# Selective scan's step: other places for products, sums, du and the pieces beside

## The chip, the cores and the metric

The kernel runs on one core of a Trainium2 chip. The core has five engines that work side by side, each through its own queue in order: TensorE (PE, matmuls), VectorE (DVE), ScalarE (ACT), GpSimd (POOL) and SyncE (SP, which only issues DMAs here). The metric is the time of one execution on the device, in microseconds (us). A profile of one execution lists the instructions of every engine with start, duration and the event that ended the idle time before each.

## The reference, cut to what matters

Eight images of 64 x 64 x 96 pass four layers. Layers 0 and 2 are selective scans (the subject here), layer 1 is a scan in chunks, layer 3 a resampling with a small network ("slow layer" in the kernel). The core of layers 0 and 2, for four directions (k) over the L = 4096 points, 192 channels (d) and 16 states (n):

```python
delta = softplus(dts + dt_projs_bias)
def step(h, inp):
    ut, dt, bt, ct = inp
    dA = jnp.exp(dt[..., None] * A4)
    dBu = (dt * ut)[..., None] * bt[:, :, None, :]
    h = h * dA + dBu
    y = jnp.einsum('bkdn,bkn->bkd', h, ct)
    return (h, y)
```

Directions 1 and 3 read the image transposed, directions 2 and 3 backwards; the four y are added.

## The kernel before

`selective_scan` cuts a direction into 8 chunks of 512 points, so a layer has 32 steps (direction, chunk). A step has six units (n = 0 to 5) of 32 channels. In a unit's tiles the 128 partitions are 32 channels x 4 states, and four groups of 512 points (the other states) lie behind each other: 2048 elements per partition. Units 0 to 2 hold channels 0 to 95 (half 0), units 3 to 5 the others. There are 8 images x 2 layers x 32 steps = 512 steps.

What a unit needs, by function:

- `spread` (L821): PE copies one unit's 32 rows of du = delta * u onto the 128 partitions, into the PSUM tile pu (one buffer, tag "misc").
- `with_b` (L828): db = pu * B. Units 0, 1, 3, 4 on DVE from pu; units 2 and 5 on POOL from du2, a copy of du that comes by DMA.
- `decays` (L840): ACT makes exp(delta * A) for two groups into PSUM tile da0 or da1 (p = 0, 1).
- `scan` (L854): DVE's scan over two groups, from da and db to h. It frees da for the next unit's decays.
- `leave` (L871): ACT saves the last column as state, POOL multiplies h by C in place. `enter` (L811): ACT puts the earlier state into db.
- `total_y` (L885): PE adds, for the three units of a half, over the partitions: first the earlier y (or the skip term, L890), then 12 products with `red` (L900), each to 32 of 96 columns by q. ACT copies the result to y (L1001 or L1011).

`prepare` (L720) makes the tiles of a step ahead, as a generator that `prepare_part` moves on by one part: pv on PE (L733); ACT's copy to raw (L738); pv on PE (L743); copy (L747), DMA bcd, and the four DMAs that make b; softplus on ACT and two DMAs dd; four DMAs dx of half 0 and four of c; du on POOL (L785 transposed, L791 else), DMA dud and four DMAs du2; dx of half 1. `Beside` (L619) runs the slow layer of the image before as pieces: `begin` issues a piece's matmuls into a PSUM tile, `end` has ACT take it away. There are 119 pieces in layer 0 and 116 in layer 2, so 3 or 4 per step (`quota`), from the second image on. The first image has none. Both pv, the sums and most pieces share one PSUM tile, tag "py".

The order is written out by hand in the loop over t from L971: what stands there is the order in each engine's queue. Before, DVE's order over a step was (S for a scan, B for a product): unit 0 S S B, units 1 and 2 S S, S S B, unit 3 S S B, unit 4 S S, unit 5 S S B. `with_b` for units 2 and 5, on POOL, follows the first scan two units earlier. Each sum of y was issued whole (at n = 0 for units 3 to 5 of the step before, at n = 3 for units 0 to 2), in this order:

```python
for g in range(NSG):
    for q in range(3):
        nc.tensor.matmul(
            turn_back(py[32 * q : 32 * q + 32, :], wh, LC), red, cut(hs[q][:, g, :], wh),
            start=False, stop=(g == NSG - 1))
```

## Time and profile before

| | |
|---|---|
| median of 3 runs | 26653.47 us (26631.27 to 26673.9) |
| the profiled execution | 26693.06 us, its span 26691.2 us |
| mean granted TensorE clock | 0.794 |
| instructions | 282273 |
| ACT, L847 (decays), 12288 | 8478.8 us busy, 690 ns each |
| DVE, L832 (with_b), 2048 | 4643.3 us busy, 2267 ns each |
| POOL, L785 and L791 (du), 256 each | 2885 and 2381 ns each |
| PE, L826 (spread), 4096 records | 2940.8 us busy, 805 ns each |
| DMA | 2836.59 MB, mean 106 GB/s |

A group's line in the profile names line, engine, operation, output and inputs with their shapes and the number of instructions; behind the bar stand the busy time of the group, the mean duration of one in ns, and the idle time of the engine before them with what ended it. In PE's groups 128*32 means active rows * columns. PEclk is the share of the full TensorE clock that was granted. In a timeline each row is start, duration, engine, line, operation and tiles; SPq rows are issues of DMAs.

### The profile page before, as it was taken

Reading aid. Unit: us, or ns where it says so; the run is one execution under the profiler, and the core shown is the slowest. Engines: PE = TensorE matmul, PEld = TensorE weight load, DVE = VectorE, ACT = ScalarE, POOL = GpSimd, SP = SyncE. Lnnn points to the kernel's source line nnn. Section 1 sums busy time; section 2 is a strip of 40 time slices with the busy share of each in tenths; the row PEclk is TensorE's granted clock in tenths of the full one; section 3 lists DMA queues with packets and bytes.
Section 4 is the critical chain, followed back from the end, with each engine's and each line's share of the span. In section 5 each row is a group of like instructions: output and inputs, shape, how many; then the busy total and the mean of one; then the engine's idle time right before and its main releaser. Section 6 shows DMA issues by size and latency. Waiting matters only on the chain. (4 is left out here: it accounts for less than half of the span.)

```text
span 26691.2 us, 282273 instructions
## 1 busy us (share of the span) xinstructions
PE 21984.9 (82%) x90981; PEld 8484.0 (32%) x90981; DVE 23982.3 (90%) x16689; ACT 16407.9 (61%) x29921; POOL 21235.6 (80%) x7928
## 2 busy tenths in 40 slices
PE   6796788888888878888888887888888888788888
PEld 2151222422224222242223422234222342223424
DVE  9989999898998989889898898988989889898896
ACT  5656566565665656556565565655656556565564
POOL 8949898497975979759797697976979769796694
PEclk7787777877778777787778877788777887778878
DMA  5515454154541545425453254532545325453352
GB/s 125 122 35 129 120 129 109 41 132 123 131 107 47 131 123 132 102 50 133 123 132 97 58 132 123 133 90 62 132 123 132 85 68 133 123 133 78 75 132 68
DMA packets 1678115, 2836.59 MB, mean 106 GB/s; under 512 B 434473, under 2 KB 477769, under 8 KB 1672033
## 3 DMA queue, kind: packets, MB, share of 16 engines
q1 hardware_dynamic: 1660000, 2812.23, 43.3%
q8 instruction: 731, 11.98, 0.2%
q10 hardware_dynamic: 16640, 6.29, 0.1%
q14 instruction: 744, 6.09, 0.1%
HBM read 2390.02 MB, written 427.49 MB: 106 GB/s over the span
## 5 line engine op out<-in xcount | busy, mean ns | idle before, releaser
L862 DVE TENSOR_TENSOR_SCAN h<-da,db 128x1026 f32<-128x1026 f32 x6144 | 13745.7, 2281 | 744.8 <-ACT da L847 378.5
L883 POOL TENSOR_TENSOR h<-h,c 128x2048 f32<-128x2048 f32 x3072 | 12743.1, 4172 | 968.2 <-ACT state L878 528.3
L900 PE MATMUL py<-h,cst 128*32 128x512 f32 x24576 | 5344.6, 749 | 473.0 <-POOL h L883 472.6
L847 ACT ACTIVATE da<-dx,a0s 128x512 f32<-128x512 f32 x6144 | 4239.6, 690 | 1548.8 <-DVE h L862 1373.0
L847 ACT ACTIVATE da<-dx,a2s 128x512 f32<-128x512 f32 x6144 | 4239.2, 690 | 1546.5 <-DVE h L862 1375.0
L832 POOL TENSOR_TENSOR db<-du,b 128x2048 f32<-128x2048 f32 x1024 | 4661.3, 4552 | 306.7 <-DMA du<-dud 226.5
L832 DVE TENSOR_TENSOR db<-pu,b 128x2048 f32<-128x2048 f32 x2048 | 4643.3, 2267 | 141.6 <-PE pu L826 138.2
L826 PE MATMUL pu<-du,cst 32*128 32x512 f32 x4096 | 2940.8, 805 | 1455.7 <-DVE db L832 927.4
L900 PEld LDWEIGHTS py<-h,cst 128*32 128x32 f32 x24576 | 1217.5, 133 | 4997.2 <-issue 3829.7
L826 PEld LDWEIGHTS pu<-du,cst 32*128 32x128 f32 x4096 | 735.2, 223 | 3145.9 <-DVE db L832 1580.8
L743 PE MATMUL pv<-u,wk 96*128 96x512 f32 x2048 | 1290.5, 762 | 388.1 <-ACT raw L738 388.1
L506 PE MATMUL ps<-s,w3as 96*128 96x512 f32 x1344 | 1069.4, 888 | 641.7 <-ACT sf L513 258.9
L1349 ACT ACTIVATE sg<-sg 128x768 f32<-128x768 f32 x1024 | 819.6, 800 | 862.2 <-PE sg L1333 862.2
L890 PE MATMUL py<-y,cst 96*96 96x512 f32 x1536 | 1306.1, 946 | 9.0 <-ACT y L1011 5.7
L733 PE MATMUL pv<-u,wk 96*96 96x512 f32 x2048 | 1200.9, 716 | 59.6 <-DVE u L281 27.4
L1303 POOL TENSOR_TENSOR ce<-ec,cr 112x512 f32<-112x512 f32 x256 | 521.5, 2037 | 754.9 <-ACT ec L1301 736.6
L1381 DVE TENSOR_TENSOR wt<-wt,cbm 128x768 f32<-128x768 f32 x1024 | 990.6, 1001 | 128.9 <-ACT wt L1350 128.1
L878 ACT COPY state<-h 128x4 f32<-128x4 f32 x3072 | 588.6, 192 | 796.5 <-DVE h L862 788.2
L526 PE MATMUL ps<-w3bs,sf 128*128 128x96 f32 x5376 | 1071.5, 356 | 0.0
L314 POOL TENSOR_SCALAR xn<-xs,sb 96x512 f32<-96x512 f32 x192 | 204.8, 1069 | 997.9 <-PE pz L319 440.8
L526 PEld LDWEIGHTS ps<-w3bs,sf 128*128 128x128 f32 x5376 | 992.9, 270 | 0.0
L738 ACT COPY raw<-pv 96x512 f32<-96x512 f32 x512 | 297.6, 581 | 970.1 <-PE pv L733 943.5
(238 smaller groups left out, 29900.9 us busy)
## 6 DMA issues: line engine op xcount, KB each, us to landing
dx<-dd SPq DMA_DIRECT2D x4096, 192.0 KB
b<-bcd SPq DMA_DIRECT2D x2048, 256.0 KB
c<-bcd SPq DMA_DIRECT2D x2048, 256.0 KB
du<-dud SPq DMA_DIRECT2D x2048, 128.0 KB
dd<-raw SPq DMA_DIRECT2D x1024, 192.0 KB
dud<-du SPq DMA_DIRECT2D x512, 128.0 KB
xd<-xs SPq DMA_DIRECT2D x256, 192.0 KB
cr<-bcd SPq DMA_DIRECT2D x1536, 32.0 KB
```

The source lines that it names most:

```text
L506: nc.tensor.matmul(ps, w3as[:, m * 128 : (m + 1) * 128], live["x2"], start=True, stop=True)
L526: nc.tensor.matmul(po, live["f"][m][:, at : at + 128], w2q[:, m, :], start=False, stop=(m == 2),)
L733: nc.tensor.matmul(pv[:DM], weights[k][:, hi, 128:], uv[hi], start=(hi == 0), stop=(hi == 1))
L743: nc.tensor.matmul(pv, weights[k][:, hi, :128], uv[hi], start=(hi == 0), stop=(hi == 1))
L826: nc.tensor.matmul(pu, sel[rows, :], m["du"][rows, n // 3, :], start=True, stop=True)
L832: (nc.gpsimd if pool else nc.vector).tensor_mul(groups(m["db", n]), (m["du2"][:, n // 3, :] if pool else m["pu"]) .unsqueeze(1) .to_broadc ...
L847: nc.scalar.activation(dst[:, g, :LC], made[i]["dx"][n // 3][:, n % 3, :], AF.Exp, scale=av4[:, k, n, gs : gs + 1],)
L862: nc.vector.tensor_tensor_scan(made[i]["h", n][:, at][:, way], das[p][:, rev : 2 * SEG + rev][:, way], made[i]["db", n][:, at][:, way], 0. ...
L883: nc.gpsimd.tensor_mul(h, h, made[i]["c"])
L890: nc.tensor.matmul(py, skip[:, hf, :] if k == 0 else ident[:DM, :DM], near((u if k == 0 else y)[:, hf, :], wh, c * LC, LC), start=True, st ...
L900: nc.tensor.matmul(turn_back(py[32 * q : 32 * q + 32, :], wh, LC), red, cut(hs[q][:, g, :], wh), start=False, stop=(g == NSG - 1),)
L1381: nc.vector.tensor_mul(it["wt"], it["wt"], m["cbm"][:, j : j + 1, :].to_broadcast([128, RK, Q]),)
```

## The change

`prepare` gets one more `yield`, between du and its DMAs (dud, du2), and so has nine parts. du is computed in unit 2 (`leave(t, n == 2)`), its DMAs are issued at the end of unit 5. `with_b` can do half of the groups. The loop is written anew: in every unit a product, or half of one, stands between the two scans (unit 0: B of unit 1; units 1 and 2: the halves for unit 3; unit 3: B of unit 4; units 4 and 5: the halves for the next unit 0). POOL's products for units 2 and 5 come first in units 0 and 3. `total_y` becomes a generator with the loops over q and g changed about: q = 0 and 1 are issued first, at the start of units 0 and 3, q = 2 after a `spread` later in the same unit. The sum's copy stands before `decays` in units 1 and 4. The pieces beside are begun and ended elsewhere, now all in the "py" tile; softplus stands in the middle of unit 0, the first pv at the end of unit 4 with its copy.

```diff
@@ -790,6 +790,7 @@
                 else:
                     nc.gpsimd.tensor_mul(du, raw[:DM], u[:, :, at : at + LC])
                 m["du"] = du
+                yield
                 dud = dp.tile([32, 2, LC], F32, name="dud")
                 nc.sync.dma_start(dud, du[64:96])
                 m["du2"] = du2 = tp.tile([128, 2, LC], F32, name="du2")
@@ -825,16 +826,17 @@
                 m["pu"] = pu = pmp.tile([128, LC], F32, name="pu", tag="misc")
                 nc.tensor.matmul(pu, sel[rows, :], m["du"][rows, n // 3, :], start=True, stop=True)
 
-            def with_b(t):
+            def with_b(t, part=slice(None)):
 
                 m, n = made[t // units], t % units
                 pool = n % 3 == 2
+                out, b = groups(m["db", n])[:, part], m["b"][:, part]
                 (nc.gpsimd if pool else nc.vector).tensor_mul(
-                    groups(m["db", n]),
+                    out,
                     (m["du2"][:, n // 3, :] if pool else m["pu"])
                     .unsqueeze(1)
-                    .to_broadcast([128, NSG, LC]),
-                    m["b"],
+                    .to_broadcast([128, out.shape[1], LC]),
+                    b,
                 )
 
             def decays(t, p):
@@ -894,18 +896,20 @@
                     start=True,
                     stop=False,
                 )
-                hs = [groups(made[i].pop(("h", 3 * hf + q))) for q in range(3)]
-                for g in range(NSG):
-                    for q in range(3):
+                for q in range(3):
+                    h = groups(made[i].pop(("h", 3 * hf + q)))
+                    for g in range(NSG):
                         nc.tensor.matmul(
                             turn_back(py[32 * q : 32 * q + 32, :], wh, LC),
                             red,
-                            cut(hs[q][:, g, :], wh),
+                            cut(h[:, g, :], wh),
                             start=False,
                             stop=(g == NSG - 1),
                         )
+                    if q == 1:
+                        yield
                 py = py.rearrange("p (h w) -> p h w", h=64) if wh else py
-                return near(y[:, hf, :], wh, c * LC, LC), py
+                yield near(y[:, hf, :], wh, c * LC, LC), py
 
             going = {}
 
@@ -943,7 +947,7 @@
                 prepare_part(0)
             conv_half(5, 1, pmp, "misc")
             conv(w, y, u, (8, 24), 0)
-            for _ in range(2):
+            for _ in range(3):
                 prepare_part(0)
             conv_half(6, 0, pyp, "py")
             for t in range(3):
@@ -967,65 +971,91 @@
                 prepare_part(1)
             conv(w, y, u, (40, 48), 0)
             with_b(0)
+            spread(1)
             other = Beside(ops)
+            low, high = slice(0, 2), slice(2, 4)
             for t in range(total + 2):
                 n, i = t % units, t // units
-                ahead = t + 1 < total
+                live, ahead = t < total, t + 1 < total
+                if t >= total:
+                    if n == 0:
+                        adding = total_y(i - 1, 1)
+                        next(adding)
+                        sums = next(adding)
+                    else:
+                        nc.scalar.copy(*sums)
+                    continue
                 quota = (i + 1) * len(ops) // len(steps) - i * len(ops) // len(steps)
-                if n == 2 and quota > 1:
+                assert quota <= 4
+
+                if n == 0:
+                    with_b(t + 2)
+                    if i > 0:
+                        adding = total_y(i - 1, 1)
+                        next(adding)
+                elif n == 3:
+                    adding = total_y(i, 0)
+                    next(adding)
+                elif n == 5:
+                    prepare_part(i + 2)
+                scan(t, 0)
+                if n == 1 and t > 1:
+                    nc.scalar.copy(*sums)
+                elif n == 4:
+                    nc.scalar.copy(*sums)
+                if ahead:
+                    decays(t + 1, 0)
+                if n == 0:
+                    with_b(t + 1)
+                    prepare_part(i + 1)
+                elif n == 1:
                     other.begin(pyp, "py")
-                if n in (0, 3) and ahead:
-                    spread(t + 1)
-                elif n == 1 and t + 2 < total:
+                    with_b(t + 2, low)
+                elif n == 2:
+                    other.end()
+                    with_b(t + 1, high)
                     spread(t + 2)
-                if n == 0 and i > 0:
-                    sums = total_y(i - 1, 1)
+                    if quota > 3:
+                        other.begin(pyp, "py")
                 elif n == 3:
-                    sums = total_y(i, 0)
+                    with_b(t + 2)
+                    with_b(t + 1)
+                    if t + 3 < total:
+                        spread(t + 3)
+                    sums = next(adding)
                 elif n == 4:
-                    if quota > 3:
-                        other.begin(pmp, "misc")
+                    if quota > 2:
+                        other.begin(pyp, "py")
                     if t + 2 < total:
+                        with_b(t + 2, low)
+                elif n == 5:
+                    prepare_part(i + 2)
+                    if ahead:
+                        with_b(t + 1, high)
                         spread(t + 2)
+                scan(t, 1)
+                if n == 0:
+                    spread(t + 3)
+                    if i > 0:
+                        sums = next(adding)
+                elif n in (1, 4):
+                    other.end()
+                leave(t, n == 2)
+                if ahead:
+                    decays(t + 1, 1)
+                if n == 2:
+                    other.end()
+                if t + 3 < total:
+                    enter(t + 3)
+                if n == 1:
+                    if quota > 1:
+                        other.begin(pyp, "py")
+                    prepare_part(i + 1)
+                elif n == 4:
+                    prepare_part(i + 2)
                     prepare_part(i + 2)
                 elif n == 5:
-                    prepare_part(i + 2)
-                if t < total:
-                    scan(t, 0)
-                    if n % 3 == 0 and t + 2 < total:
-                        with_b(t + 2)
-                if ahead:
-                    decays(t + 1, 0)
-                if n == 1:
-                    if t > 1:
-                        nc.scalar.copy(*sums)
-                    if t < total:
-                        other.begin(pyp, "py")
-                elif n == 2:
-                    other.end()
-                    if quota > 2:
-                        other.begin(pyp, "py")
-                elif n == 3:
-                    other.end()
-                elif n == 4:
-                    nc.scalar.copy(*sums)
-                    other.end()
-                if t < total:
-                    scan(t, 1)
-                    leave(t, n == 3)
-                if t + 3 < total:
-                    enter(t + 3)
-                if ahead:
-                    decays(t + 1, 1)
-                    if (n + 1) % 3 != 2:
-                        with_b(t + 1)
-                if n in (1, 2):
-                    other.end()
-                    if n == 2 and quota > 4:
-                        other.begin(pyp, "py")
-                if n in (4, 5):
-                    prepare_part(i + 2)
-                if n in (0, 1, 5):
+                    prepare_part(i + 1)
                     prepare_part(i + 1)
             other.flush()
             assert other.at == len(ops)
```

## The prediction

> **What bounds the kernel now.** I read the page's busy line and its groups first.
>
> ```profile
> PE 21984.9 (82%) x90981; PEld 8484.0 (32%) x90981; DVE 23982.3 (90%) x16689; ACT 16407.9 (61%) x29921; POOL 21235.6 (80%) x7928
> ...
> L862 DVE TENSOR_TENSOR_SCAN h<-da,db 128x1026 f32<-128x1026 f32 x6144 | 13745.7, 2281 | 744.8 <-ACT da L847 378.5
> L883 POOL TENSOR_TENSOR h<-h,c 128x2048 f32<-128x2048 f32 x3072 | 12743.1, 4172 | 968.2 <-ACT state L878 528.3
> L900 PE MATMUL py<-h,cst 128*32 128x512 f32 x24576 | 5344.6, 749 | 473.0 <-POOL h L883 472.6
> ...
> L832 POOL TENSOR_TENSOR db<-du,b 128x2048 f32<-128x2048 f32 x1024 | 4661.3, 4552 | 306.7 <-DMA du<-dud 226.5
> ```
>
> There are 512 steps of six units. From first scan to first scan of the next step they are 36.25 us apart in the first image's two scan layers (64 steps, no pieces beside) and 37.4 in the other fourteen (448 steps). DVE works 12 scans at a pitch of 2.24 and 4 products at 2.25 = 35.9 us per step. POOL works 6 x 4.13 + 2 x 4.5 + 2.85 (L785) or 2.33 (L791) = 36.6 or 36.1, mean 36.35. DVE's idle time before L862 and L832 is 744.8 + 141.6 = 886 us in all. So the best that any reordering can do is POOL's mean: 448 x (37.4 - 36.35) = 470 us. PE is not the bound, but its price is what the change alters, so I read two more views. The timeline of PE's weight loads and matmuls over one sum of y:
>
> ```profile
> 1028.84 3.62 PE L900 MATMUL py<-h,cst 128*32 128x512 f32 x20 [2.37 <-POOL h L883]
> ...
> 1030.16 0.12 PEld L900 LDWEIGHTS py<-h,cst 128*32 128x32 f32 x3 [0.31 <-issue]
> 1030.59 0.12 PEld L900 LDWEIGHTS py<-h,cst 128*32 128x32 f32 x3 [0.31 <-issue]
> 1031.02 0.11 PEld L900 LDWEIGHTS py<-h,cst 128*32 128x32 f32 x1 [0.31 <-issue]
> 1031.45 0.11 PEld L900 LDWEIGHTS py<-h,cst 128*32 128x32 f32 x1 [0.32 <-issue]
> ```
>
> Each product has two records (24576 over 512 x 24). Three records, one for each q and its 32 columns, start together every 0.43 us. Two of the q had run ahead here while the third waited for h, and so the last loads come singly: still 0.43 us apart. Three side by side cost what one alone costs. The second view is windows of 3.41 us, the grid on which the trace's clock changes:
>
> ```profile
> core 0: us, PE busy (x) PEld busy (x) DVE busy (x) ACT busy (x) POOL busy (x), PEclk, DMA share, GB/s
> 1006.46:1009.87 3.41, 3.41 (x7) 0.59 (x8) 3.41 (x2) 1.38 (x2) 3.41 (x2) 0.50 1.01 220
> 1009.87:1013.28 3.41, 3.41 (x15) 0.77 (x12) 3.31 (x3) 1.58 (x4) 3.41 (x1) 0.50 0.03 5
> 1013.28:1016.70 3.42, 1.91 (x13) 0.49 (x8) 3.42 (x3) 1.90 (x3) 3.42 (x3) 1.00 0.00 0
> ...
> 1061.07:1064.48 3.41, 3.41 (x5) 0.88 (x4) 3.37 (x3) 2.26 (x7) 3.41 (x2) 0.50 0.08 19
> 1064.48:1067.90 3.42, 3.42 (x11) 0.54 (x13) 3.32 (x2) 3.36 (x6) 3.42 (x2) 0.50 0.59 172
> 1067.90:1071.31 3.41, 3.41 (x23) 0.81 (x17) 3.22 (x3) 3.35 (x5) 3.41 (x2) 1.00 0.82 189
> ```
>
> PE is busy throughout the first two and the fourth and fifth. Only the second and fifth, where three L900 ran at a time, are followed by full clock; the first and fourth held mainly L826 (32 rows) and L890. I counted all 7812 such windows, weighting each matmul by active rows x columns over 128 x 128. At half clock, none of 125 windows that one stream filled, but with under 45% of the array, was followed by full clock; 46% of those at 54 to 62% were, and 99% above 74%. At full clock, 71% of the 38 filled by one stream of about a quarter of the array kept it. At half clock everything doubles: such loads are then 0.85 us apart.
>
> **The change, part by part.**
>
> *Products.* Two of four DVE products per step become halves. A half costs between 1.13 (half of L832's 2.27) and 1.21 us (L333, 1024 elements from PSUM); I take 1.18, nearest to L333. Two splits add 0.2 us, so DVE has 36.1, hidden under POOL's 36.35. Uncovered: 100 us over 512 steps. Evenly spread products give ACT at least 3.4 us between the scans that it serves instead of 2.24; this is what could win the 470 us.
>
> *du and its DMAs.* du moves on POOL from before unit 3's product to before unit 2's, so that db of unit 5 comes one du (2.85) later. Its DMAs do not follow: dud and du2 (5 issues) move from unit 3 to the end of unit 5, on SP behind bcd and b of the step after. The SP timeline:
>
> ```profile
> 1016.42 0.31 SPq L794 DMA_DIRECT2D dud<-du  x1
> 1018.38 1.71 SPq L797 DMA_DIRECT2D du<-dud  x4
> 1023.50 0.30 SPq L749 DMA_DIRECT2D bcd<-raw  x1
> 1025.14 1.74 SPq L756 DMA_DIRECT2D b<-bcd  x4
> 1026.93 1.84 SPq L774 DMA_DIRECT2D dx<-dd  x4
> ```
>
> From the copy of raw (1022.9) to the issue of b is 2.24 us; b's 1.05 MB passes until 1031.2, 6.05 after its issue. dud now passes behind it and is there after some 7.0; du2 takes 3.4 more (the last bytes at 1021.7). On SP, dud now waits until ACT has copied raw and bcd has landed; behind it stand du2, dx of units 3 to 5, both dd and the next dx and c, and POOL waits for du2 alone. So du2 lands 2.24 + 10.4 = 12.6 us after that copy, and POOL's db of unit 2 waits for it, with h of units 0 to 2 and db of unit 5 behind it. This closes a loop: db 4.53, h 4.13, h, du 2.85, h, db 4.53 = 24.3; scan of unit 5 2.27; decays 1.5; copy to du2 12.6: 40.6 us (40.1 with L791). Lower bound of this cost: nothing, if another wait is longer (below); upper: 40.35 - 36.25 = 4.1 us per step. Fewer DMAs ahead of it can't gain: du2 was 7 us early before.
>
> *Sums of y in two parts.* The loops over q and g change places. Four products of one q now follow each other on the same 32 columns: eight records, one stream. Three q overlap only where one ends and the next begins: 22 pitches instead of 8. At full clock 9.4 us instead of 3.4; at half clock 22 x 0.853 = 18.8. Spread of the pu for unit 3 (and unit 0) stands on PE between part one and part two, and the sum's copy stands on ACT before decays, which a scan awaits. Part two waits on PE for POOL's h of the third unit, and the pieces, both pv and every later spread stand behind it; DVE's products wait for these spreads. The single space py, which sums, pieces and both pv share, makes PE and ACT take turns. So I add up the turn of one step at half clock: two sums x (skip, L890, 2.0 + 18.8 + 0.72 for the copy, as long as PE idles for a copy of L738) = 43.0; four L826 x 2.0 = 8.0; L733 3.6, L743 3.78 and two copies = 8.8; 3.67 pieces (235 in 64 steps) x (2.3 + copy 0.9) = 11.7. A piece's 2.3 is the mean over a set of seven: L487 1.7, three L506 at 2.08, two of L522 with L526 at 3.5, L545 1.2. Sum: 71.5 us with pieces. Without them 59.8, and 5 us in which PE, its next instruction being the spread of unit 4, waits for unit 3's second half (decays 1.5, scan 2.24, half 1.18): 64.8. At full clock: 22.4 + 4 + 5.4 + 9.2 = 41.0, with 3 us of waits for POOL's h and for ACT's order 44; without pieces the du2 loop (40.6) and 1.1 for part two behind h of unit 2: 41.7. Lower bound of a sum's price: nothing (no serial run of three q is in the trace, only the single loads at 1031); upper: 15.4 us more than before at full clock's 3.4.
>
> *The clock.* A quarter of the array cannot release it. What can: L743 (75% of the array for 3.78 us), when a window lies over about three quarters of it: 45% of the steps; and one mixing piece per step (L526, 128*128), about 40%. Held some 4 windows (1 / 0.29, and the first), 13.7 us, each saving as much: with pieces 71.5 - 0.87 x 13.7 = 59.6 (0.45 and, for the piece, 0.42 releases per step); without 64.8 - 0.45 x 13.7 = 58.6.
>
> *The rest.* Softplus goes to the middle of unit 0, where ACT has 3 us free; pieces move to py and a third one may stand before the first sum. Both are in the turns above.
>
> Sum: 26691 + 448 x (59.6 - 37.4) + 64 x (58.6 - 36.25) = 26691 + 9946 + 1430 = 38067, against the profiled span; the median of the runs is 38 us below it, and I do not correct for that.
>
> The Trainium skill speaks differently of the clock: "TensorE: Matmul & The Clock Gate", section "Part 1: The HAM clock gate", says "The warm-up budget is ~3.4 µs of time, not a number of matmuls", so a PE that is always busy would be at full clock. By that the sum would be the first rival's 30000. The row of 1061.07 is against it: 3.41 us busy, and half clock after it.
>
> **Rivals.** (1) Full clock nearly always: 448 x (44 - 37.4) + 64 x (41.7 - 36.25) = 3306, so 30000. For it: 71% of narrow windows kept full clock once they had it. Against: the 125. (2) PE overlaps the q whatever the order, and only du2 is late: 448 x (40.35 - 37.4) + 64 x 4.1 = 1584, 28280. Against: the single loads at 1031. (3) Faster: the overlap stays and du2 lands before POOL wants it (5.9 us into the step, when h of the step before is done); then POOL's 36.35 decides, 26230. It turns once du2 lands over 6 us into the step; by the chain it lands near 10. For it: idle 886 us to win. (4) Always half clock: 448 x 34.1 + 64 x 28.55 = 17104, 43800; part of the forecast's upper end.
>
> **How the numbers follow.** Forecast 0.76 (own range 33500 to 42500, from half the steps' work at full clock to nearly none), rival 1 0.12, rival 2 0.06, rival 3 0.05, no change 0.01. Predicted: 38070. The range takes in most of rival 1: 29500 to 42000. A run of this kernel tells 0.2% from no change: faster 0.05, same 0.02, slower 0.93.
>
> **What would show it.** L900's successor single, 0.43 or 0.85 us apart, its busy time two to four times 5344.6 us; granted clock in the scan layers falling from 0.74 to 0.76 to near 0.6; PE above 90% busy; DVE idle before scans of units 2 and 5, ended by the sum's copy and decays. Scans with a wait for POOL's db, and that for du2, would be rival 2; L900 in threes would make the prediction wrong, and clock above 0.85 would make it rival 1.

## The result: 1.18 times the time, at a higher clock

The changed kernel takes 31449.31 us (median, 31443.76 to 31455.24) against 26663.69 us for the kernel before in the same session: ratio 1.1796, 95% interval 1.1775 to 1.1816, that is 4786 us more. The profiled execution's span is 31450.2 us. The forecast had the sign and the size was wrong: 38070 us were forecast. The range held the time only because it took in most of the first rival's. The granted clock, which was to fall to near 0.6 in the scan layers, rose: its mean is 0.855 for 0.794.

A step now takes 43.9 us in the first image's two scan layers and 47.0 in the others (36.25 and 37.4 before). The page's busy line and groups:

```profile
PE 25459.4 (81%) x90981; PEld 9073.0 (29%) x90981; DVE 23976.6 (76%) x17697; ACT 16505.1 (52%) x29921; POOL 21217.5 (67%) x7928
...
L864 DVE TENSOR_TENSOR_SCAN h<-da,db 128x1026 f32<-128x1026 f32 x6144 | 13835.9, 2279 | 3604.5 <-POOL db L834 2460.6
...
L902 PE MATMUL py<-h,cst 128*32 128x512 f32 x24576 | 9977.1, 631 | 29.2 <-POOL h L885 27.6
L834 POOL TENSOR_TENSOR db<-du,b 128x2048 f32<-128x2048 f32 x1024 | 4624.0, 4516 | 4571.8 <-DMA du<-dud 2010.4
L834 DVE TENSOR_TENSOR db<-pu,b 128x1024 f32<-128x1024 f32 (+1 forms) x3056 | 4797.5, 1570 | 2093.2 <-PE pu L827 1654.6
```

DVE, POOL and ACT do the same work in the same busy time as before; only PE has more (25459 for 21985 us), since the sums' products no longer overlap (9977 for 5345 us). What has grown on DVE is idle time: 3604.5 us ahead of scans and 2093.2 ahead of products, 886 in all before. The waits (engine and line, awaited engine and line; total us, times, longest) name who ended it:

```profile
ACT y L1005 <- PE py L902: 3585.3, 512, 10.1
...
DVE h L864 <- POOL db L834: 2460.6, 477, 7.8
...
POOL db L834 <- DMA du<-dud: 2010.4, 211, 19.7
POOL db L834 <- ACT da L849: 1866.3, 214, 11.0
...
DVE db L834 <- PE pu L827: 1654.6, 567, 6.0
```

The scan of unit 2 waits for POOL's product, that for du2; DVE's products wait for spreads; and ScalarE waits in each step for the sum of y (at L1005; at L1003, the other copy, 1085.8 us more). The line that puts POOL's wait down to da is du2's as well. The profile names the last of several events; but in five steps in a row from 1052.73 on, three of which name da, the product starts 0.33 or 0.34 us after du2's last part has landed by the trace's semaphores (1096.42 for 1096.76), wherever ACT stands. And when du2 alone is issued earlier (a2 below), the first line falls to 247.0 us and the second is gone. The timeline of one sum of units 0 to 2 (start, duration, engine, line; in brackets the idle time before and what ended it):

```profile
1064.74 7.47 PE L902 MATMUL py<-h,cst 128*32 128x512 f32 x16
...
1065.60 0.18 PEld L902 LDWEIGHTS py<-h,cst 128*32 128x32 f32 x1 [0.68 <-issue]
1066.45 0.18 PEld L902 LDWEIGHTS py<-h,cst 128*32 128x32 f32 x1 [0.68 <-issue]
...
1069.90 0.11 PEld L902 LDWEIGHTS py<-h,cst 128*32 128x32 f32 x1 [0.32 <-issue]
1070.33 0.11 PEld L902 LDWEIGHTS py<-h,cst 128*32 128x32 f32 x1 [0.32 <-issue]
...
1073.19 3.62 PE L902 MATMUL py<-h,cst 128*32 128x512 f32 x8
```

PEld rows are loads of weights. They are single, 0.85 us apart, as forecast, then 0.43 apart: the clock turned to full in the middle of a run of single streams of 32 columns. That is what the forecast had excluded. And the chain around du2:

```profile
1052.73 4.50 POOL L834 TENSOR_TENSOR db<-du,b 128x2048 f32<-128x2048 f32 x1 [8.07 <-DMA du<-dud]
...
1060.82 2.04 PE L827 MATMUL pu<-du,cst 32*128 32x512 f32 x2 [10.36 <-DVE db L834]
...
1065.42 2.36 POOL L791 TENSOR_TENSOR du<-raw,u 96x1024 f32<-96x1024 f32 x1
...
1071.87 4.52 POOL L834 TENSOR_TENSOR db<-du,b 128x2048 f32<-128x2048 f32 x1
...
1076.85 0.58 ACT L1005 COPY y<-py 96x512 f32<-96x512 f32 x1 [5.75 <-PE py L902]
...
1078.85 2.29 DVE L864 TENSOR_TENSOR_SCAN h<-da,db 128x1026 f32<-128x1026 f32 x1 [2.07 <-ACT da L849]
...
1082.85 0.58 ACT L747 COPY raw<-pv 128x512 f32<-128x512 f32 x1 [0.25 <-PE pv L743]
...
1085.21 1.73 SPq L756 DMA_DIRECT2D b<-bcd  x4
...
1086.98 0.43 SPq L795 DMA_DIRECT2D dud<-du  x1
...
1092.41 1.71 SPq L798 DMA_DIRECT2D du<-dud  x4
...
1096.76 4.50 POOL L834 TENSOR_TENSOR db<-du,b 128x2048 f32<-128x2048 f32 x1 [7.76 <-ACT da L849]
```

du is ready at 1067.78, but its DMA dud stands in SP's queue behind bcd, which waits for the copy of raw, and b, and is issued 19.2 us later; du2 can be issued only 5.43 us after that, when dud has landed. POOL's product starts 13.91 us after the copy of raw. From one such product to the next it is 44.03 us: the loop that the prediction drew is closed, and sets the step in this layer. (In the layers with pieces it was not followed term by term.)

### The profile page after: what moved, and what is told of

Same layout as the page of the kernel before. It is cut to its first block, busy times and chain, and to the rows that moved or that the text cites. A ratio compares the mean times of both kernels' runs of the same rounds, so it can differ in the third digit from the quotient of the medians.

```text
span 31450.2 us, 284888 instructions
## 1 busy us (share of the span) xinstructions
PE 25459.4 (81%) x90981; PEld 9073.0 (29%) x90981; DVE 23976.6 (76%) x17697; ACT 16505.1 (52%) x29921; POOL 21217.5 (67%) x7928
## 5 line engine op out<-in xcount | busy, mean ns | idle before, releaser
L864 DVE TENSOR_TENSOR_SCAN h<-da,db 128x1026 f32<-128x1026 f32 x6144 | 13835.9, 2279 | 3604.5 <-POOL db L834 2460.6
L902 PE MATMUL py<-h,cst 128*32 128x512 f32 x24576 | 9977.1, 631 | 29.2 <-POOL h L885 27.6
L834 POOL TENSOR_TENSOR db<-du,b 128x2048 f32<-128x2048 f32 x1024 | 4624.0, 4516 | 4571.8 <-DMA du<-dud 2010.4
L834 DVE TENSOR_TENSOR db<-pu,b 128x1024 f32<-128x1024 f32 (+1 forms) x3056 | 4797.5, 1570 | 2093.2 <-PE pu L827 1654.6
L827 PE MATMUL pu<-du,cst 32*128 32x512 f32 x4096 | 2817.7, 773 | 3241.3 <-DVE db L834 3240.9
L902 PEld LDWEIGHTS py<-h,cst 128*32 128x32 f32 x24576 | 2274.9, 115 | 7877.9 <-issue 7577.3
L1005 ACT COPY y<-py 96x512 f32<-96x512 f32 x512 | 297.5, 581 | 3585.3 <-PE py L902 3585.3
L743 PE MATMUL pv<-u,wk 96*128 96x512 f32 x2048 | 1079.2, 652 | 404.4 <-ACT raw L738 404.4
L733 PE MATMUL pv<-u,wk 96*96 96x512 f32 x2048 | 1052.1, 638 | 376.6 <-ACT sf L513 127.7
L506 PE MATMUL ps<-s,w3as 96*128 96x512 f32 x1344 | 969.8, 811 | 383.8 <-ACT y L1003 117.4
L526 PE MATMUL ps<-w3bs,sf 128*128 128x96 f32 x5376 | 885.9, 310 | 0.0
L1363 PE MATMUL sg<-rr,lr 32*128 32x384 f32 x4096 | 853.1, 523 | 17.4 <-POOL rr L1310 15.1
L1003 ACT COPY y<-py 96x512 f32<-96x512 f32 x496 | 288.3, 581 | 1085.8 <-PE py L902 1085.8
```

Source lines behind the costliest of these rows:

```text
L506: nc.tensor.matmul(ps, w3as[:, m * 128 : (m + 1) * 128], live["x2"], start=True, stop=True)
L526: nc.tensor.matmul(po, live["f"][m][:, at : at + 128], w2q[:, m, :], start=False, stop=(m == 2),)
L733: nc.tensor.matmul(pv[:DM], weights[k][:, hi, 128:], uv[hi], start=(hi == 0), stop=(hi == 1))
L743: nc.tensor.matmul(pv, weights[k][:, hi, :128], uv[hi], start=(hi == 0), stop=(hi == 1))
L827: nc.tensor.matmul(pu, sel[rows, :], m["du"][rows, n // 3, :], start=True, stop=True)
L834: (nc.gpsimd if pool else nc.vector).tensor_mul(out, (m["du2"][:, n // 3, :] if pool else m["pu"]) .unsqueeze(1) .to_broadcast([128, out.s ...
```

## The experiments

Ratios are to the kernel before of the same session, with 95% intervals. In the text, "wait for pu" and "wait for da" are DVE's, ahead of products and of scans. The clock is that of the profiled execution.

| kernel | us | ratio | clock |
|---|---|---|---|
| changed | 31449.31 | 1.1796 [1.1775, 1.1816] | 0.855 |
| before, du2 behind b (b2) | 31173.29 | 1.1688 [1.167, 1.1707] | 0.744 |
| before, sums with q outside (b1) | 27845.08 | 1.0444 [1.0429, 1.046] | 0.844 |
| changed, q side by side (a1) | 31231.17 | 1.1714 [1.1697, 1.1732] | 0.814 |
| changed, du2 before b (a2) | 29222.44 | 1.0961 [1.0944, 1.0977] | 0.883 |
| a1 and a2 (a3) | 28380.2 | 1.0647 [1.0629, 1.0665] | 0.854 |
| a3, sum's copy after decays (a4) | 27858.38 | 1.0441 [1.0424, 1.0458] | 0.860 |
| a4, enter before decays (a5) | 27745.98 | 1.0404 [1.0388, 1.0419] | 0.859 |
| a5, spread before the whole sum (a6) | 28646.73 | 1.0737 [1.0721, 1.0753] | 0.817 |
| a5, piece taken earlier (a7) | 27726.68 | 1.0396 [1.038, 1.0411] | 0.860 |
| a5, fourth piece in unit 5 (a8) | 27514.85 | 1.0332 [1.0306, 1.0357] | 0.875 |
| before, products moved (b3) | 28543.23 | 1.0691 [1.0677, 1.0706] | 0.761 |
| b3 without halves (b4) | 28420.78 | 1.0655 [1.064, 1.0669] | 0.764 |
| b3, three spreads moved (b5) | 28525.47 | 1.0697 [1.0682, 1.0712] | 0.759 |

### The place of du2's DMAs, alone and undone

b2 is the kernel before with one edit of the change: dud and du2 are issued at the end of unit 5.

```diff
                 m["du"] = du
+                yield
                 dud = dp.tile([32, 2, LC], F32, name="dud")
...
                 if n in (0, 1, 5):
                     prepare_part(i + 1)
+                if n == 5:
+                    prepare_part(i + 1)
```

> The kernel before, with nothing changed but dud and du2: issued at the end of unit 5, behind bcd and b of the step after. Theory A: the copy of raw to POOL's db took 13.9 us in the changed kernel; here the copy stands behind unit 5's last decays, so that a step is scan of unit 2 to the end of unit 5's 22.5, decays and copy 2.2, 13.9 and db 4.5 = 43 us: 29000 to 30000 us, DVE's wait for POOL's db before unit 2's scan over 2500 us. If du2 were late only together with the serial sums: within 1% of 26660.

31173 us: this edit alone makes a slowdown nearly as large as the whole change's, more than expected. The wait ahead of scans, and the same queue as in the changed kernel's timeline:

```profile
DVE h L863 <- POOL db L833: 4495.8, 485, 12.1
...
1046.46 1.73 SPq L756 DMA_DIRECT2D b<-bcd  x4
1048.28 0.37 SPq L795 DMA_DIRECT2D dud<-du  x1
...
1053.93 1.71 SPq L798 DMA_DIRECT2D du<-dud  x4
...
1058.46 4.50 POOL L833 TENSOR_TENSOR db<-du,b 128x2048 f32<-128x2048 f32 x1 [11.87 <-DMA du<-dud]
```

dud's issue to du2's issue: 5.65 us behind b. In the profile before, with nothing in front, it was 1.96 (1016.42 to 1018.38), and dud was issued as soon as du was done: SP stood there waiting for POOL's du. a2 undoes the place in the changed kernel: the part with dud and du2 runs at the end of unit 4, ahead of bcd and b.

```diff
                 elif n == 4:
+                    prepare_part(i + 1)
                     prepare_part(i + 2)
                     prepare_part(i + 2)
                 elif n == 5:
                     prepare_part(i + 1)
-                    prepare_part(i + 1)
```

> The changed kernel, with dud and du2 issued at the end of unit 4, before bcd and b of the step after instead of behind them. Theory A: POOL finds du2 landed, DVE's wait of 2460 us for POOL's db goes; the serial sums still hold unit 4's product and unit 5's scan, and what unit 2 no longer waits for, it partly waits for in the sum's copy: 28800 to 30000 us. If du2 were not the cause of that wait, but POOL's own load, the time would stay within 1% of 31450. Theory B: below 30500 only if the clock rises too.

29222 us, 2227 less. The wait of scans for POOL's product is gone from the waits, and so is POOL's own ahead of its products (4571.8 us in the changed kernel, both of the lines above in it):

```profile
L834 POOL TENSOR_TENSOR db<-du,b 128x2048 f32<-128x2048 f32 x1024 | 4636.1, 4527 | 305.6 <-DMA du<-dud 247.0
```

What went is hardly the time behind other bytes. SP's wait at du2's issue for dud to land, first in the changed kernel, then in a2, where dud stands behind dx and c:

```profile
SPq L798 <- DMA dud<-du: 2545.1, 512, 6.9
```

```profile
SPq L798 <- DMA dud<-du: 2182.6, 512, 7.3
```

It is 5.0 us per step and still 4.3 in a2. So the larger part of what a2 gives back is that dud no longer stands in the queue behind an issue whose input, the copy of raw, comes late; no run separates the two exactly. The clock rose too (0.883), which theory B had allowed for; a1 and b1 below decide against it. What is left of DVE's waits:

```profile
DVE db L834 <- PE pu L827: 1605.8, 540, 6.0
DVE h L864 <- ACT da L849: 1366.2, 937, 5.2
```

### The sums, alone and undone

b1 is the kernel before with nothing but the two loops of the sum changed about, so that q is outside.

```diff
-                for g in range(NSG):
-                    for q in range(3):
+                for q in range(3):
+                    for g in range(NSG):
```

> The kernel before, with nothing changed but the loops of a sum: q outside, g inside, so 12 products run one after the other by columns. Theory A (rows set the clock): granted clock at or above 0.84, busy time of the sums' line near 10000 us, time 26700 to 28200, since the last unit's four products end as early as before and only PE's total grows. Theory B: granted clock near 0.6, time above 33000.

27845 us and a clock of 0.844, as theory A had them (the sums' busy time is less than it expected). Its groups, and a line of its waits:

```profile
L862 DVE TENSOR_TENSOR_SCAN h<-da,db 128x1026 f32<-128x1026 f32 x6144 | 13775.5, 2282 | 2023.1 <-ACT da L847 1629.0
...
L900 PE MATMUL py<-h,cst 128*32 128x512 f32 x24576 | 8333.5, 641 | 13.6 <-POOL h L883 13.1
...
ACT y L1011 <- PE py L900: 1368.1, 462, 4.8
```

Single streams cost 8333.5 us where three side by side cost 5344.6, mostly at full clock, and 1184 us of the time: DVE now waits 1629 us for da, whose decays stand behind the sum's copy, at which ScalarE waits. a1 does the opposite in the changed kernel: in part one q = 0 and 1 alternate.

```diff
-                for q in range(3):
-                    h = groups(made[i].pop(("h", 3 * hf + q)))
+                hs = [groups(made[i].pop(("h", 3 * hf + q))) for q in range(3)]
+                for qs in ((0, 1), (2,)):
                     for g in range(NSG):
...
-                    if q == 1:
+                        for q in qs:
...
+                    if len(qs) == 2:
                         yield
```

> The changed kernel, with the loops of part one of a sum changed back: q = 0 and 1 side by side, group by group, then q = 2 alone after the spread. Theory A (two new waits at full clock: serial sums, and du2 late behind b): part one takes 8 pitches instead of 15, 3 us less; DVE's waits before unit 4's half product (3 us per step for pu) and before unit 5's scan mostly go, the wait of unit 2's scan for POOL's db (4.8 us) stays: 28700 to 29500 us. The clock, if active rows times streaming time set it, falls from 0.855 to 0.80 to 0.83, because PE streams for less time. Theory B (the forecast's: streams on 32 columns hold the clock at half): the clock rises above 0.855 and the time falls below 28700.

The time is a miss: 31231 us, 218 less. The sums' busy time falls by 1394 us, and the clock with it (0.814), as theory A had it, where theory B wanted a rise. But the scans' wait for POOL's product stays (2502.5 us): what the sums save lies beside the wait for du2. a3 makes both edits.

> Both edits together. Theory A: nothing of the two waits is left; products between the scans then show what they are worth: 26300 to 27200 us, DVE idle before scans and products under 1500 us. If a third cause is in the change (the copy before decays, enter behind decays, pieces in one PSUM tile), the time stays above 27500.

28380 us: with du2 early, the same edit is worth 842 us (29222 to 28380). But the time missed the expected 26300 to 27200, so there was more: a wait for da of 1156.6 us and one for pu of 1111.2.

### ScalarE's order

a4 puts the sum's copy behind decays in units 1 and 4, as it stood before the change; a5 also puts enter ahead of decays, as it stood.

```diff
                 scan(t, 0)
+                if ahead:
+                    decays(t + 1, 0)
                 if n == 1 and t > 1:
                     nc.scalar.copy(*sums)
                 elif n == 4:
                     nc.scalar.copy(*sums)
-                if ahead:
-                    decays(t + 1, 0)
```

> The kernel of both edits (sums side by side, du2 before b), with the sum's copy on ACT put behind decays of the next unit, as it stood before the change, in units 1 and 4. Theory A, with a third cause: that copy waits on ACT up to 6.4 us for part two of the sum and holds decays, so unit 5's scan waits (903 us in that run): 27300 to 27900 us. If the copy only shows the lateness of PE, which then appears as a longer wait for pu or for a piece's copy, the time stays above 28100.

```diff
                 leave(t, n == 2)
+                if t + 3 < total:
+                    enter(t + 3)
                 if ahead:
                     decays(t + 1, 1)
                 if n == 2:
                     other.end()
-                if t + 3 < total:
-                    enter(t + 3)
```

> As the run before it, and enter put ahead of decays on ACT, as it stood before the change. Theory A, fourth cause: unit 3's first half product waits for db's first column, which ACT writes after decays (372 us in the run with both edits): 250 to 400 us less than the run before it. Rival: the next wait (PE's pu for unit 3) takes its place, less than 100 us.

The copy is worth 522 us, enter 112, a miss. In a layer without pieces the time from first to last scan is now 1155.3 us (1157.0 before the change, 1401 in it): there nothing of the loss is left, and nothing was gained. The rest, some 1080 us, lies in the layers with pieces: 39.8 us per step for 37.4. There DVE waits 700 us for pu ahead of the half product between unit 4's scans, and a6 puts that spread ahead of the whole sum:

```diff
-                elif n == 3:
-                    adding = total_y(i, 0)
-                    next(adding)
...
                         spread(t + 3)
+                    adding = total_y(i, 0)
+                    next(adding)
                     sums = next(adding)
```

> As the run before it, and in unit 3 the spread for the next unit 0 goes to PE ahead of the whole sum instead of between its parts. Theory A, fifth cause: unit 4's half product waits for pu behind part one (790 us with pieces in the run with both edits): below 26900 us, and if nothing else is left, faster than the kernel before at 26300 to 26650. Rival: POOL, with du and db of unit 5 ahead of h, takes over, and the time stays at or above 26900.

A miss, 901 us slower. The wait for pu fell from 1141.5 to 570.1 us in all; the wait for da rose from 744.9 to 1471.6, and 810.3 us of scans waiting for PE's sum were new, since the sum, issued later, keeps the h that they write. So of these two places for the sum, the two parts around the spread are the better one, once q = 0 and 1 run side by side.

### The products alone

b3 is the kernel before with the products moved between the scans, and nothing else; b4 has no halves (unit 3's product stands whole in unit 2).

```diff
+                if n in (0, 3, 5) and ahead:
+                    with_b(t + 1)
+                elif n == 1 and t + 2 < total:
+                    with_b(t + 2, slice(0, 2))
+                elif n == 2 and ahead:
+                    with_b(t + 1, slice(2, 4))
                 if t < total:
                     scan(t, 1)
...
                     decays(t + 1, 1)
-                    if (n + 1) % 3 != 2:
-                        with_b(t + 1)
```

> The kernel before with nothing of the change but the moved products: with_b of unit 1 stands whole between the scans of unit 0, the halves for unit 3 between those of units 1 and 2, unit 4's between those of unit 3, the next unit 0's whole between those of unit 5; sums, pieces, du and its DMAs stay as before. Theory (the products were worth having and other parts of the change lost it): POOL's 36.35 us per step becomes the bound, 36.3 us per step without pieces and 36.5 to 37.2 with them instead of 37.4: 26250 to 26600 us, ratio 0.985 to 0.998. Rival (the products move is itself a loss: a scan waits for spread or for enter where it did not): over 26800 us. If it is 26600 to 26750 the 886 us of DVE's idle time were not to be won by products at all.

> As the run with the products only, but without halves: with_b of unit 3 stands whole between the scans of unit 2. Theory: the two splits per step cost 0.2 us of DVE, which POOL's 36.35 hides, so the time agrees with that run within 60 us; 26250 to 26600. Rival (DVE with splits is the bound in the layers with pieces): up to 512 x 0.2 = 100 us faster than that run.

Both missed: 28543 and 28421 us. The move of the products costs 1847 us by itself, the other way round from what was expected. DVE's products in b3:

```profile
L833 DVE TENSOR_TENSOR db<-pu,b 128x2048 f32<-128x2048 f32 (+1 forms) x2560 | 4739.3, 1851 | 2564.6 <-PE pu L826 2489.6
```

141.6 us of idle time have become 2564.6, nearly all for pu. b4's wait for pu is 1299.2 us, and its scans wait for da and h instead (950.4 and 301.7), so the 122 us between the two don't price the splits. b5 moves three spreads ahead:

```diff
-                if n in (0, 3) and ahead:
-                    spread(t + 1)
-                elif n == 1 and t + 2 < total:
-                    spread(t + 2)
...
+                if n == 0 and t + 3 < total:
+                    spread(t + 3)
+                elif n in (2, 5) and t + 2 < total:
+                    spread(t + 2)
                 if t < total:
                     scan(t, 1)
```

> The run with the products only lost 1847 us, and the profile shows where: VectorE waits 2489.6 us for pu, the copy that TensorE makes for each product, above all in unit 3. This kernel is that one with three spreads moved ahead as the change has them (unit 1's in unit 5 of the step before, unit 3's in unit 0, unit 4's in unit 2); the next unit 0's stays where it was, and sums, pieces, both pv, du and its DMAs stay as before. Theory P (the products are worth nothing by themselves but cost nothing either, once their spreads are ahead of the sums; what the change still loses after its sums, du2 and ScalarE's order are mended comes from the new places of the pieces and pv): under 26850 us, wait for pu under 500 us. Theory Q (a product between the scans needs its pu half a unit earlier than TensorE's turn with pieces and sums can give it, wherever the spreads stand): 27300 to 28300, with over 1000 us of waiting for pu left, nearly all of it in the layers with pieces.

28525 us, no gain, 2485.2 us of waiting for pu left, nearer theory Q but above its range. The timeline ahead of the product between unit 3's scans, where DVE waits longest for pu, shows why the new places changed nothing there:

```profile
7328.97 2.07 PE L506 MATMUL ps<-s,w3as 96*128 96x512 f32 x2 [4.89 <-ACT y L999]
...
7331.82 2.08 PE L506 MATMUL ps<-s,w3as 96*128 96x512 f32 x2 [0.78 <-ACT sf L513]
...
7334.67 2.08 PE L506 MATMUL ps<-s,w3as 96*128 96x512 f32 x2 [0.78 <-ACT sf L513]
...
7336.68 2.07 PE L826 MATMUL pu<-du,cst 32*128 32x512 f32 x2
...
7338.79 2.29 DVE L833 TENSOR_TENSOR db<-pu,b 128x2048 f32<-128x2048 f32 x1 [2.49 <-PE pu L826]
```

Three pieces stand ahead of the spread in PE's queue, each waiting until ScalarE has emptied py of the one before. But pieces are not all of it. In the first image's layers, which have none, b5 takes 38.9 us per step for 36.25, and DVE waits some 207 us for pu over the 64 steps, 3.2 us each (5.1 with pieces). There it is the half product between unit 1's scans, whose spread stands behind a whole sum that waits for POOL's h:

```profile
1057.87 3.63 PE L901 MATMUL py<-h,cst 128*32 128x512 f32 x20 [2.47 <-POOL h L884]
...
1061.43 1.12 PE L826 MATMUL pu<-du,cst 32*128 32x512 f32 x2
...
1062.64 1.23 DVE L833 TENSOR_TENSOR db<-pu,b 128x1024 f32<-128x1024 f32 x1 [2.78 <-PE pu L826]
```

So a product half a unit earlier seems to need the sums in two parts and the pieces elsewhere. That the changed kernel's larger rewriting is the price of the products' move, and not an addition to it, is a reading: no run moves the pieces or splits the sums in the kernel before.

### The pieces

a7 takes a piece begun in unit 2 away ahead of decays; a8 begins the fourth piece of a step in unit 5, not in unit 2. Both start from a5.

```diff
-                elif n in (1, 4):
+                else:
                     other.end()
...
-                if n == 2:
-                    other.end()
```

> The changed kernel with its sums, du2's DMAs and ScalarE's order mended (the run with the enter first, 27746 us), and one more edit: a piece begun in unit 2 is taken away by ScalarE right after the second scan of unit 2 is issued, ahead of decays, so that the space py comes free for the sum of unit 3 some 2 us earlier. Theory (what is left of the loss, 1080 us, is the pieces' turn on py ahead of the sum and the spread of unit 3): VectorE's wait for pu between the scans of unit 4 falls from 700 us to under 400, time 27300 to 27550. Rival (the piece's own chain is the delay, ScalarE now stands for it ahead of decays): 27700 to 28200, and the second scans wait longer for da.

```diff
                     spread(t + 2)
-                    if quota > 3:
-                        other.begin(pyp, "py")
...
                         with_b(t + 1, high)
                         spread(t + 2)
+                    if quota > 3:
+                        other.begin(pyp, "py")
...
-                if n == 2:
+                if n == 5:
                     other.end()
```

> The same 27746 us kernel, with the fourth piece of a step begun between the scans of unit 5 and taken away at that unit's end, and none begun in unit 2 any more. Theory (the fourth piece ahead of the sum of unit 3 holds PE and py there): the wait for pu between the scans of unit 4 falls below 200 us of 700, and the time to 27000 to 27400 if nothing comes back in unit 0. Rival (py has no free turn for a fourth piece: the same wait moves to unit 1's product, behind the sum of unit 0): 27600 to 28100, with over 500 us of waits for pu in units 0 and 1 (411 before).

a7 changes the time by 19 us: the wait at unit 4 fell from 700 to 474, short of the expected 400, and the scans' wait for da rose from 745 to 842. a8 gains 231 us, between the two theories: the wait at unit 4 falls to 71 as the theory had it, and the one at unit 1 rises from 114 to 474 as the rival had it. All waits of a8 for pu and da:

```profile
DVE h L864 <- ACT da L849: 800.5, 1048, 5.8
DVE db L834 <- PE pu L827: 754.8, 465, 5.8
```

So a fourth piece ahead of a sum delays whichever spread comes after it. That its place matters is shown; that py has no free turn for it is the reading that fits, not a proof. Some 840 us of a8's time over the kernel before stay unassigned beyond "in the layers with pieces, waiting for pu and da". No version that ran beats the kernel before.

### The clock by itself

The last kernel leaves the whole computation out and runs bursts of 40 matmuls of 512 columns, two records each, of seven shapes.

```python
for rows, cols in PHASES:
    ...
    for i in range(40):
        nc.tensor.matmul(ps[:cols], cst[:rows, :cols], rhs[:rows], start=(i == 0), stop=(i == 39))
```

> All of the computation is left out: x is copied to out, then TensorE runs seven bursts of 40 matmuls of 512 columns each, with (active rows, columns) = (128,32), (32,128), (64,128), (96,96), (96,32), (32,32), (128,128), after pauses of some 27 us of VectorE's work. Theory (the clock is released by windows of 3.41 us counted as active rows / 128 x time of streaming, at about 0.72): 128x32, 96x96, 96x32 and 128x128 go to full clock after one or two windows, 32x128, 64x128 and 32x32 stay at half clock for their whole burst. Rival (rows x columns counts, as in the prediction): 128x32, 96x96 (0.56), 96x32 and 32x32 stay at half clock, 128x128 alone is released. Second rival (any busy window counts): all seven are released.

Its matmuls by shape (active rows * columns; busy us, mean ns), and windows over two of the bursts, 64 x 128 and then 96 x 32 (start and end, length, PE busy with its matmuls, then PEclk, DMA share and GB/s):

```profile
L118 PE MATMUL ps<-rhs,cst 64*128 64x512 f32 x80 | 68.6, 1059 | 16.7 <-DVE rhs L115 16.7
L118 PE MATMUL ps<-rhs,cst 32*128 32x512 f32 x80 | 68.6, 1058 | 16.7 <-DVE rhs L115 16.7
...
L118 PE MATMUL ps<-rhs,cst 96*32 96x512 f32 x80 | 37.5, 633 | 16.7 <-DVE rhs L115 16.7
L118 PE MATMUL ps<-rhs,cst 96*96 96x512 f32 x80 | 37.2, 629 | 16.7 <-DVE rhs L115 16.7
L118 PE MATMUL ps<-rhs,cst 128*32 128x512 f32 x80 | 36.4, 618 | 169.9 <-DVE rhs L115 169.9
```

```profile
308.00:377.00 69.00, 68.63 (x80) 0.50 0.00 0
...
447.00:452.00 5.00, 4.47 (x6) 0.50 0.00 0
452.00:485.00 33.00, 33.00 (x75) 0.98 0.00 0
```

64 rows by 128 columns, half the array, stay at half clock through 68.63 us of unbroken work. 96 rows by 32 columns, less than a fifth of the array, go to full clock after some 6 us (the 4.47 us up to 452 and, by the 0.98 of the 33 us behind, about 1.4 more). 96 by 96 is like 96 by 32; 32 by 32 (68.5 us) is like 32 by 128. 128 by 32 began at full clock and kept it, so it shows only the keeping. In these seven shapes rows count and columns don't: both rivals fall.

With that in mind I counted the windows of 3.41 us of the two main profiles anew, weighting the time in which any matmul streams by active rows / 128. A matmul is taken to stream for its pitch, 0.43 us for 512 columns at full clock and 0.85 at half; counted over its whole modelled time, the windows at half clock with 0.72 to 0.80 turn in some 29% (before) and 47% (after) only, so that the limits hang on the way of counting:

| weight | at half clock, turned to full: before, after | weight | at full clock, kept it (both) |
|---|---|---|---|
| 0.64 to 0.72 | 4%, 10% | below 0.32 | some 3% |
| 0.72 to 0.80 | 80%, 87% | 0.32 to 0.40 | some 50% |
| 0.80 and over | 100%, 100% | 0.40 and over | 98 to 100% |

## Why the prediction was wrong, point by point

**The clock: the step that failed.** "A quarter of the array cannot release it." It can: 128 rows by 32 columns are a full row weight. The count by rows x columns couldn't tell few columns from few rows. Counted anew, the windows at half clock that one stream filled with under 45% of the array have row weights of some 0.30 to 0.64, through L826 and its 32 rows; none held 128-row products alone, so the rule was read from windows that had nothing to say about them. The row of 1061.07 is one of these. From this false premise came 71.5 us of turns at half clock and 59.6 per step, 15.6 above the same turns at full clock. Single streams keep PE busier with 128 rows, so the clock rose, in b1 too (0.844). The Trainium skill's rule that was set aside ("TensorE: Matmul & The Clock Gate", section "Part 1: The HAM clock gate": a budget of time, not of matmuls) came nearer, though the 64-row burst was busy for twenty times 3.4 us and never released; there the measurement decides.

**The first rival's size.** With full clock it gave 44 and 41.7 us per step; 47.0 and 43.9 were measured, so 30000 for 31449. In the layers without pieces the loop of du2 was 40.1 by its terms and measured 44.03, and the timeline gives each: POOL's db to the end of unit 5's db 23.66 (23.8 with L791), scan 2.29 (2.27), to the copy of raw 1.71 (1.5), copy to du2 13.91 (12.6), and a term that the sum lacked, 2.46 from POOL's db to the scan of unit 5. There the sum's copy (1076.85) stands ahead of decays, and the scan waits for da (the row of 1078.85). So in this step the loop does not run through POOL's h and db of unit 5, which end at 1076.39, but through PE, whose work ends last: from 1060.82 spread, skip, part one of the sum (7.47, more than half of it at half clock), spread and part two (3.62, from 1073.19), and then the copy. The prediction kept du2's loop and PE's turn apart as two candidates for the longest wait; here they are one loop.

**du and its DMAs.** Mechanism right: queued behind b, with POOL, the scans and the next copy in a loop. Its weight was not seen. It was called hidden behind PE's turn ("Lower bound of this cost: nothing, if another wait is longer"), but alone it costs 4500 us (b2), and in the changed kernel 2227 can be had back by its place alone (a2): about half of it lies beside the other waits, not all. "Scans with a wait for POOL's db, and that for du2" was listed as rival 2's mark, and it is the largest wait of scans.

**The sums.** Single loads 0.43 and 0.85 us apart: right, and so 22 pitches for 8 (the busy time is 1.87 times what it was; 2 to 4 had been forecast). Their price was first hidden by du2's wait (218 us in a1) and showed when that was gone (842 us, a3 against a2, with q = 2 still alone; 1184 in b1, where all three are serial). The copy ahead of decays, named in one sentence, is 522 us.

**The products.** "This is what could win the 470 us": in no run did it. Without pieces POOL's 36.35 was already met (36.25), and with or without them the products want their pu earlier than PE's queue gives it (b3, b5). The 0.2 us of the splits was not tested cleanly.

**Where 4786 us went**, in the order in which the edits were undone, which another order would share out differently: du2's place 2227, q = 0 and 1 serial 842, the sum's copy 522, enter 112, the fourth piece 231, and 850 unassigned in the layers with pieces. PE above 90% busy was wrong (81%).

## What to carry to other kernels

A transfer that something waits for should not stand in a queue behind one whose input comes late: moved there, dud went out 19.2 us after du was ready and closed a loop through the whole step. A single edit in the kernel before shows the price (4500 us) that the full change half hides. Undo suspects together as well as one by one: the sums' edit was worth 218 us behind a longer wait and 842 without it. Before a share of the array is taken as the weight of a matmul, separate rows and columns with data that vary one at a time.

## What the runs showed of the hardware that was not expected

- The clock goes by active rows x time of streaming, whatever the columns: 96 x 32 gets full clock after some 6 us, 64 x 128 not in 68.6. In windows of 3.41 us, counted as above, the turn up lies at a weight of some 0.72, the loss of full clock at some 0.36.
- A kernel can be 18% slower at a higher clock (0.855 for 0.794), and b2 17% slower at a lower one (0.744): the mean clock says how busy PE's rows were, not how fast the kernel is.
- Four transfers of du2 behind 1.05 MB of b were issued 5.4 to 5.7 us after dud, for 1.96 with nothing in front. By itself that need not cost anything: in a2 it is still 4.3 us per step behind dx and c, and POOL does not wait.
